# Deformable layer: the 7x7 offset convolution by even and odd columns with a shared sum

## The chip, the core and the metric

The kernel runs on one core of a Trainium2 chip. The metric is the device time of one execution in microseconds (us). A core has four computing engines with a queue each: TensorE (PE: matmuls, with weight loads shown apart as PEld), VectorE (DVE), ScalarE (ACT) and GpSimd (POOL); the transfers here are issued by SyncE (SP) and run on 16 DMA engines. The engines run in parallel and wait for each other by semaphores.

## The reference

A net of four layers on x of shape (8, 384, 32, 32), all float32: a Mamba layer, a deformable convolution layer, a second Mamba layer with an MLP, and a layer of shifts with a small depthwise convolution. Each adds its result to its input. The change is in the second, which (cut) computes:

```python
def deform_block(x, ow, ob, dw, pw, pb, K):           # x: 8 x 128 x 32 x 32
    offsets = conv2d(x, ow, ob, K // 2)               # K*K taps -> 2*K*K channels
    out = deform_depthwise(x, offsets, dw, K, K // 2) # sampled bilinearly at tap + offset
    return conv2d(out, pw, pb, 0)
c3, c5, c7 = split(group_norm(x), 3, axis=1)
out = concatenate([deform_block(c, ..., K) for c, K in ((c3, 3), (c5, 5), (c7, 7))], axis=1)
x = x + out * se_weight(out, fc1_w, fc2_w)
```

For K = 7 `conv2d` is a sum over 49 taps of a 128 x 98 weight matrix by the image moved by the tap, zero outside.

## The kernel before

The layers run one after the other. `deform_fast` (L918) does the deformable layer; a general version stands behind a branch on a flag (`far`) that says whether some offset was too large for the fast one.

For each of 8 samples it goes through three blocks, K = 3, 5, 7. A block has its taps in groups of four ("quads") and one single tap, each in two halves of the rows: 6, 14 and 26 units, 46 a sample. A unit samples by matmuls: ACT builds from the positions the bilinear weights ("hats": `fhx`, `fhy`, `unit_hats`), DVE multiplies them into `fsm` (L1387, a ring of five buffers) and weighs the transposed image into `fxk` (L1370, `unit_dve`), and PE adds 16 products (or 4) into `wacc`[...] (L1417, `unit_pe`).

The order of PE, DVE and ACT is written out by hand, in slots, one for each unit. In slot u there stand, in this order: the positions that SP loads for unit u+4 (if it is a first half); what `put` has filed under `act0`, `pe0`, `dve0`; `begin` at a block's first unit (zeroes `wacc`); PE's products of unit u interleaved with DVE's weighing and products of unit u+1; ACT's hats of unit u+2; and what is filed under `act1`, `dve1`, `pe1`. SP's and POOL's orders are left to a scheduler. Slots are numbered from 0 to 45 within a sample here: K = 3 is 0 to 5, K = 5 is 6 to 19, K = 7 is 20 to 45.

`block_steps` (L1033) files the rest of the work. What matters here:

- The offset convolution (`conv`, L1094) of K = 7 makes two halves of 16 rows x 32 columns, 49 taps each, seven taps a slot in slots 0 to 6 and 8 to 14, into `ps_off`, one bank. `offsets` (L1111), at slots 7 and 15, adds biases and grid on DVE, stores the positions to DRAM (`fposd`), and reduces maximum and minimum into `far`. For K = 3 and 5 the images lie in four and two strips of partitions, with one `offsets` each; the conv of the next sample's K = 3 is at slot 32 and of its K = 5 at slots 33 to 38.
- `load` (L1047) fetches the next sample's x into `fxn` (one buffer, all three groups) from slot 20, `stats`, `mean`, `dev`, `mean2`, `rstd` and `norm` normalize it in place in slots 22 to 31. `mean` (PE, L133) is under `pe0` of slot 25, the last of `stats` with the aggregate (L125) under `dve1` of slot 24.
- Before a block, `image` (ACT, L1147) copies its x into 4 x 8 cells (`fxc`); `cells` (DVE, L1152), four times, repeats them fourfold into `frep`; `cells_pe` (L1158) transposes them and `cells_act` (L1163) copies the result into `fxt`, a ring of six. `rows_pe` (L1133) transposes the plain rows.
- At a block's end `sums_act` (L1169 to L1172) closes `wacc` and copies two of its banks to `fdsb` on ACT, `sums` (L1177) adds the others on DVE, and only then may `begin` (L1298) zero `wacc` again. `pe0` stands between them.
- After a sample `residual` and `scale` load x into `fxr` (one buffer), add the scaled result and store it (L1227, L1231, L1232), in three parts.

Of the kernel before, what the change touches and what calls it, by code (L numbers as in the profile page):

```python
# [8 lines left out]
F32 = mybir.dt.float32  # L9
AF = mybir.ActivationFunctionType  # L10
ALU = mybir.AluOpType
AX = mybir.AxisListType
# [3 lines left out]
P = 128  # L16
C = 384
G = C // P
H = W = 32
L = H * W  # L20
HL = L // 2
# [18 lines left out]
NT = L // P  # L40
# [5 lines left out]
RAD = {3: 2, 5: 3, 7: 4}  # L46
CONV = {3: (4, 32, L // 4), 5: (2, 64, HL), 7: (1, P, L)}
NX = 4
NB = 5
HXN, HYN, SMN = 2080, 1792, 896  # L50


# [32 lines left out]
class Net:  # L85
# [832 lines left out]
    def deform_fast(self, src, dst):  # L918
        tc, nc, ins = self.tc, self.nc, self.ins
        with ExitStack() as ctx:  # L920
            wp = ctx.enter_context(tc.tile_pool(name="w1f", bufs=1))
# [5 lines left out]
            for g, K in enumerate(KS):  # L927
                K2, (n, st, cols) = K * K, CONV[K]
                rows = 2 * K2
                ow = wp.tile([P, K2, rows if n == 1 else st], F32, name=f"fow{K}")  # L930
                ob = wp.tile([P, 1], F32, name=f"fob{K}")
                obk = wp.tile([P, 1], F32, name=f"fobk{K}")
                grid = wp.tile([P, cols], F32, name=f"fgrid{K}")
                for t in (ob, obk, grid) + ((ow,) if n > 1 else ()):
                    nc.gpsimd.memset(t, 0.0)
                nc.sync.dma_start(out=ow[:, :, :rows], in_=ins[f"ow{K}"])
                for i in range(n):
                    r = slice(i * st, i * st + rows)
                    nc.sync.dma_start(out=ob[r], in_=ins[f"ob{K}"])
                    nc.sync.dma_start(out=obk[r], in_=ins["c_cols"][:rows, Q_K + g : Q_K + g + 1])  # L940
                    nc.sync.dma_start(out=grid[r], in_=ins["c_grid"][:rows, i * cols : (i + 1) * cols])
                nc.vector.tensor_tensor(obk, obk, ob, ALU.add)
                nq = K2 // 4
                wk = wp.tile([P, nq + 1, P], F32, name=f"fwk{K}")
                for t in range(4):
                    nc.sync.dma_start(
                        out=wk[H * t : H * (t + 1), :nq, :],
                        in_=ins[f"dw{K}"][t : 4 * nq : 4, :].partition_broadcast(H),
                    )
                nc.sync.dma_start(out=wk[:, nq, :], in_=ins[f"dw{K}"][4 * nq, :].partition_broadcast(P))  # L950
                self.f[K] = (ow, ob, obk, grid, wk)
# [23 lines left out]
            first = {}  # L975
# [18 lines left out]
            with tc.manual_schedule(engines=engines):  # L994
                for u in range(min(slots), max(slots) + 1):

                    def unit(i):
                        return units[i] if 0 <= i < len(units) else None

                    now, after, hats, grid = (unit(u + k) for k in (0, 1, 2, 4))  # L1000
# [21 lines left out]
            ps = self.psum("ps_bad", rows=1, n=1)  # L1022
# [7 lines left out]
        return bass.AP(tensor=ap.tensor, offset=ap.offset + off, ap=[list(ap.ap[0])] + [list(d) for d in dims])  # L1030


    def block_steps(self, b, g, first, put, weights, src, dst):  # L1033
        nc, K = self.nc, KS[g]
        K2, pad = K * K, K // 2
        n, st, cols = CONV[K]
        ow, ob, obk, grid, _ = self.f[K]
        pwt, pwb, f1, f2 = weights
        s = {}
        if g == 0:  # L1040
            s["sample"] = {}
        sample = s["sample"] = s["sample"] if g == 0 else self.state[b, 0]["sample"]
        s0 = first[b, g]
# [37 lines left out]
        def xg():  # L1081
            return sample["xn"][:, g, :]
# [2 lines left out]
        taps = [(0, 0)] + [  # L1085
            (y, x) for y in range(-pad, pad + 1) for x in range(-pad, pad + 1) if (y, x) != (0, 0)
        ]
        nh = 2 if n == 1 else 1
        m = HL if n == 1 else cols
        rows = m // W  # L1090
        width = 2 * K2 if n == 1 else st
        used = width * n

        def conv(h, t0, t1):  # L1094
            x3 = xg().rearrange("p (h w) -> p h w", w=W)
# [43 lines left out]
            for q in range(2):  # L1139
                nc.scalar.copy(xt[:, 4 * q : 4 * q + 4, :].rearrange("p t c -> p (t c)"), s["tr"][q])  # L1140

        def image():

            xc = s["xc"] = self.q1.tile([P, NT, NX, 4, 8], F32, name="fxc")
            x5 = xg().rearrange("p (by yl bx xl) -> p by yl bx xl", yl=4, bx=NX, xl=8)
            for yl in range(4):
                nc.scalar.copy(xc[:, :, :, yl, :], x5[:, :, yl, :, :])  # L1147

        def cells(q):
            rep = s["rep"] = self.q1.tile([P, 2 * NX, 4, 32], F32, name="frep")  # L1150
            xc = s["xc"].rearrange("p by bx yl xl -> p (by bx) (yl xl)")[:, 8 * q : 8 * q + 8, :]
            nc.vector.tensor_copy(rep, xc.unsqueeze(2).to_broadcast([P, 2 * NX, 4, 32]))  # L1152

        def cells_pe():
            s["tr"] = [self.psum("ps_t") for _ in range(2)]
            for i in range(2 * NX):
                a = s["rep"][:, i].rearrange("p t l -> p (t l)")
                nc.tensor.transpose(s["tr"][i // NX][:, i % NX * P : (i % NX + 1) * P], a, self.ident)  # L1158

        def cells_act(q):  # L1160
            xt = s[q] = self.q1.tile([P, 2 * NX, P], F32, name="fxt4", tag="fxt4", bufs=6)
            for by in range(2):
                nc.scalar.copy(xt[:, NX * by : NX * (by + 1), :].rearrange("p t c -> p (t c)"), s["tr"][by])  # L1163


        def sums_act():
            acc = s["acc"]
            for o in range(NB):
                nc.tensor.matmul(acc[:, o, :], self.zero[:, :P], self.zero, start=False, stop=True)  # L1169
            dsb = s["dsb"] = self.q1.tile([P, L], F32, name="fdsb")  # L1170
            nc.scalar.copy(dsb[:, :HL], acc[:, 0, :])
            nc.scalar.copy(dsb[:, HL:], acc[:, NB - 1, :])  # L1172

        def sums():
            for o in range(1, NB - 1):
                d = s["dsb"][:, 4 * o * W : 4 * o * W + HL]
                nc.vector.tensor_tensor(d, d, s["acc"][:, o, :], ALU.add)  # L1177
# [45 lines left out]
            nc.scalar.activation(sample["se"], sample["se"], AF.Sigmoid)  # L1223

        def residual(k):
            xr = sample["xr"] = self.q1.tile([P, L], F32, name="fxr")
            nc.sync.dma_start(out=xr, in_=src[:, k, :])  # L1227

        def scale(k):
# [3 lines left out]

        if g == 0:
            t = s0 - 2 * len(QUADS[KS[-1]])
            put(t, "act0", load)
            for i in range(G):
                put(t + 2 + i, "dve1", stats, i)
            put(t + 5, "pe0", mean)
            put(t + 5, "dve1", dev)  # L1240
            put(t + 6, "act1", square)
            put(t + 7, "pe0", mean2)
            put(t + 7, "dve1", var)
            put(t + 8, "act1", rstd)
            for i in range(G):
                put(t + 9 + i, "dve1", norm, i)
            put(t + 12, "pe1", conv, 0, 0, K2)
            put(t + 13, "dve0", offsets, 0)
        elif g == 1:
            t = first[b, 0] - 13  # L1250
            for i in range(6):
                put(t + i, "pe1", conv, 0, K2 * i // 6, K2 * (i + 1) // 6)
            put(t + 6, "dve0", offsets, 0)
        else:
            t = first[b, 0]
            for h in range(2):
                for i in range(7):
                    k = 8 * h + i
                    where = "pe0" if t + k in (first[b, 0], first[b, 1]) else "pe1"
                    put(t + k, where, conv, h, 7 * i, 7 * i + 7)  # L1260
                put(t + 8 * h + 7, "dve0", offsets, h)
        put(s0 - 4, "act0", image)
        put(s0 - 4, "pe1", rows_pe)
        put(s0 - 3, "act0", rows_act)
        put(s0 - 3, "dve0", cells, 0)
        put(s0 - 3, "pe1", cells_pe)
        put(s0 - 2, "act0", cells_act, 0)
        put(s0 - 2, "dve0", cells, 1)
        put(s0 - 2, "pe1", cells_pe)
        put(s0 - 1, "act0", cells_act, 1)  # L1270
        put(s0 - 1, "dve1", cells, 2)
        put(s0, "pe0", cells_pe)
        put(s0, "act1", cells_act, 2)
        put(s0, "dve1", cells, 3)
        put(s0 + 1, "pe0", cells_pe)
        put(s0 + 1, "act1", cells_act, 3)
        put(end, "act0", sums_act)
        put(end, "dve0", sums)
        put(end + 1, "pe1", point)
        put(end + 2, "act0", point_act)  # L1280
        put(end + 2, "dve1", squeeze)
        if g == G - 1:
            put(end + 3, "pe0", fc1)
            put(end + 3, "act1", relu)
            put(end + 4, "pe0", fc2)
            put(end + 4, "dve1", branches)
            put(end + 5, "act1", sigmoid)
            for k, t in enumerate((6, 9, 12)):
                put(end + t - 2, "act0", residual, k)
                put(end + t, "dve1", scale, k)  # L1290
        return s
# [112 lines left out]
    def unit_pe(self, b, g, j, half):  # L1404
# [344 lines left out]
```

## Time and profile before

Three runs took 9,599.3, 9,603.1 and 9,605.7 us. The profiled execution took 9,605.4 us; its trace spans 9,603.5.

| | us | what |
|---|---|---|
| median of 3 runs | 9,603.1 | |
| profiled execution / its span | 9,605.4 / 9,603.5 | mean TensorE clock 0.948 of full |
| deformable layer | about 3,058 to 5,970 | from the last store of the first layer's results |
| one sample in it | 355.3 | samples 1 to 6 lie between 355.1 and 356.7 |
| PE / DVE / ACT / POOL busy | 8,576 / 8,106 / 6,509 / 5,760 | over the span |

How to read it: the page has busy shares in 40 slices of 240 us, then groups of instructions by source line (busy us, mean ns of one, and the idle time before them with what ended it). A float32 matmul stands as two records, each with its own weight load. Matmuls overlap their neighbours, so their durations add up to more than the time they take; the time from one start to the next is what counts in a full queue. In the windows a row gives a stretch, its length, and the busy us and instructions of PE, PEld, DVE, ACT and POOL, then the granted clock, the DMA share and GB/s.

### The profile page before, as it was taken

How to read it: one execution, taken by the hardware profiler on the slowest of the kernel's cores; microseconds unless marked ns; L12 is line 12 of the kernel's file. 1: busy time of each engine (PE TensorE's matmuls, PEld its weight loads, DVE VectorE, ACT ScalarE, POOL GpSimd, SP SyncE). 2: the span in 40 equal slices, each digit the busy share in tenths (PEclk: the TensorE clock that was granted, in tenths of full speed). 3: DMA queues.
4: the chain of work that ended last, by engine and by line, in shares of the span. 5: the costliest groups of instructions: out<-in, count | busy, mean ns of one | idle time of the engine just before them, and what ended most of it. 6: DMA issues, size and time to landing. Idle time of an engine off the chain costs nothing. (4 is left out here: it accounts for less than half of the span.)

```text
span 9603.5 us, 87989 instructions
## 1 busy us (share of the span) xinstructions
PE 8576.2 (89%) x28252; PEld 4549.0 (47%) x28252; DVE 8106.0 (84%) x8807; ACT 6509.3 (68%) x10236; POOL 5760.4 (60%) x3788
## 2 busy tenths in 40 slices
PE   7898888888886899999999997699999999999987
PEld 2333333333332677677677676233433434433333
DVE  6999999999996678778778778699999999999983
ACT  5666666666663677777777777567777677777750
POOL 6888888888896000000000000699999999999974
PEclk8999999999998999999999999799999999999998
DMA  1211211121121233333333333233332243323336
GB/s 71 84 59 46 84 52 52 50 83 55 49 80 39 76 76 86 91 77 84 88 82 84 88 77 78 75 99 117 95 92 91 88 132 98 96 90 91 114 104 128
DMA packets 560754, 792.02 MB, mean 82 GB/s; under 512 B 238018, under 2 KB 391010, under 8 KB 536600
## 3 DMA queue, kind: packets, MB, share of 16 engines
q1 hardware_dynamic: 508056, 779.99, 27.7%
q10 hardware_dynamic: 52224, 6.30, 0.4%
q8 instruction: 225, 3.69, 0.2%
q14 instruction: 249, 2.04, 0.1%
HBM read 716.49 MB, written 69.66 MB: 82 GB/s over the span
## 5 line engine op out<-in xcount | busy, mean ns | idle before, releaser
L426 POOL TENSOR_TENSOR db<-du,bc 128x1024 f32<-128x1024 f32 x1536 | 3610.8, 2356 | 417.9 <-DVE hs L436 225.9
L436 DVE TENSOR_TENSOR_SCAN da<-da,db 128x1024 f32<-128x1024 f32 x1272 | 2912.3, 2290 | 200.3 <-ACT da L421 150.5
L467 PE MATMUL y<-hs,ident 128*128 128x512 f32 x5184 | 2613.1, 640 | 388.0 <-DVE hs L450 243.6
L421 ACT ACTIVATE da<-dt,na 128x512 f32<-128x512 f32 x3072 | 2119.9, 691 | 911.8 <-DVE hs L450 684.9
L394 POOL TENSOR_TENSOR dt<-dt,sp_e 128x512 f32<-128x512 f32 x192 | 244.1, 1271 | 3086.9 <-DVE sp_e L386 3086.9
L467 PEld LDWEIGHTS y<-hs,ident 128*128 128x128 f32 x5184 | 1019.6, 203 | 1879.1 <-issue 1142.7
L1417 PE MATMUL wacc<-fsm,fxk 128*128 128x221 f32 (+34 forms) x10624 | 1635.3, 312 | 73.3 <-DVE fsm L1387 71.5
L450 DVE TENSOR_TENSOR hs<-da,bc 128x1024 f32<-128x1024 f32 x1272 | 1557.9, 1225 | 118.5 <-PE y L467 14.1
L1417 PEld LDWEIGHTS wacc<-fsm,fxk 128*128 128x128 f32 x10624 | 1549.3, 193 | 209.2 <-DVE fsm L1387 132.5
L1387 DVE TENSOR_TENSOR fsm<-fhy,fhx 128x170 f32<-128x170 f32 (+42 forms) x3216 | 1173.2, 429 | 429.1 <-PE wacc L1417 413.7
L1347 ACT ACTIVATE fhy<-fpyx,cell 128x416 f32<-128x416 f32 (+9 forms) x1280 | 645.6, 576 | 397.7 <-DVE fsm L1387 397.7
L1105 PE MATMUL ps_off<-fxn,fow 128*32 128x248 f32 (+18 forms) x2944 | 831.8, 522 | 3.8 <-issue 2.0
L1370 DVE TENSOR_TENSOR fxk<-fxt,fwk 128x1024 f32<-128x1024 f32 (+1 forms) x688 | 786.6, 1180 | 6.4 <-ACT fxt L1163 6.4
L436 DVE TENSOR_TENSOR_SCAN hs<-da,db 128x1024 f32<-128x1024 f32 x264 | 602.4, 2282 | 69.0 <-POOL db L414 30.7
L447 POOL TENSOR_TENSOR hs<-hs,bc 128x1024 f32<-128x1024 f32 x264 | 622.1, 2357 | 36.6 <-ACT st L442 36.4
L454 POOL TENSOR_TENSOR hs<-hs 128x512 f32<-128x512 f32 x480 | 609.5, 1270 | 3.5 <-DVE hs L450 3.5
L550 PE MATMUL ps_m<-hid,wm 128*128 128x512 f32 x1152 | 536.7, 611 | 30.7 <-ACT hid L543 25.8
L528 PE MATMUL ps_h<-t,wm 128*128 128x512 f32 x1152 | 534.5, 601 | 17.0 <-DVE x L557 16.8
L1352 ACT ACTIVATE fhy<-fhy,cols 128x1344 f32<-128x1344 f32 (+10 forms) x368 | 530.7, 1442 | 12.0
L1105 PEld LDWEIGHTS ps_off<-fxn,fow 128*98 128x98 f32 (+2 forms) x2944 | 352.3, 147 | 381.6 <-issue 358.6
L442 ACT COPY st<-da 128x2 f32<-128x2 f32 x624 | 97.9, 157 | 506.3 <-DVE hs L450 504.8
L1334 ACT ACTIVATE fhx<-fpyx,cell 128x544 f32<-128x544 f32 (+8 forms) x640 | 380.1, 666 | 0.0
(192 smaller groups left out, 9453.3 us busy)
## 6 DMA issues: line engine op xcount, KB each, us to landing
bc<-bcd SPq DMA_DIRECT2D x256, 1024.0 KB
fpyx<-fposd SPq DMA_DIRECT2D x640, 256.0 KB
wm<-in_w SPq DMA_DIRECT2D x96, 768.0 KB
x<-x SPq DMA_DIRECT2D x71, 768.0 KB
winr<-in_win SPq DMA_DIRECT2D x192, 192.0 KB
x<-in_x SPq DMA_DIRECT2D x40, 768.0 KB
fpyx<-fposd SPq DMA_DIRECT2D x24, 1024.0 KB
wm<-in_wout SPq DMA_DIRECT2D x48, 384.0 KB
```

What stands on the lines that cost most here:

```text
L421: nc.scalar.activation(da[:, i, :], s["dt", j], AF.Exp, scale=na[:, j, n : n + 1])
L426: nc.gpsimd.tensor_tensor(db, du, s["bc"][m][:, 0], ALU.mult)
L436: nc.vector.tensor_tensor_scan(h1, da1, db1, 0.0, ALU.mult, ALU.add)
L447: nc.gpsimd.tensor_tensor(s["hs", m], s["hs", m], c, ALU.mult)
L450: nc.vector.tensor_tensor(hs, s["da", m], c, ALU.mult)
L454: nc.gpsimd.tensor_tensor(hs[:, 0, :], hs[:, 0, :], hs[:, 1, :], ALU.add)
L467: nc.tensor.matmul(s["y"], self.ident, s["hs", m][:, i, :], start=first and i == 0, stop=k == NU - 1 and i == n - 1,)
L1105: nc.tensor.matmul(o[:, ya - r0 : yb - r0, xa:xb], ow[:, (dy + pad) * K + dx + pad, :], x3[:, ya + dy : yb + dy, xa + dx : xb + dx], start ...
L1347: nc.scalar.activation(hy[:, at : at + (yb - ya) * W], pyx[:, 0, ya * W : yb * W], AF.Abs, bias=bias)
L1370: nc.vector.tensor_tensor(t[:, :n], x, wk[:, j : j + 1, :].to_broadcast([P, n, P]), ALU.mult)
L1387: nc.vector.tensor_tensor(self.sub(sm, at, [(r * w, n), (w, r), (1, w)]), self.sub(hy, hy_at[by] + xa, [(r * W, n), (W, r), (1, w)]), self ...
L1417: nc.tensor.matmul(a[:, ya - 4 * o : yb - 4 * o, xa:xb], k, self.sub(sm, sm_at[by], [(w, yb - ya), (1, w)]), start=False, stop=False,)
```

## The change

Write an image row as even columns e(i) = x(2i) and odd ones o(i) = x(2i+1), each 16 long. A row of seven weights on them gives two sums, for even and odd output columns, of seven half-row products each. They are rewritten with s(i) = e(i) + o(i): products of s with three weights serve both outputs, and four products with differences of weights complete the odd columns, four the even ones. Eleven products of 16 columns for each of seven tap rows, over all 32 rows at once, in three parts: 21 matmuls on the sum, 28 on odd columns, 28 on even columns of x, all into one bank in turn. After the first part ACT copies the sum with the bias to `ffs`; after each other part DVE adds it and writes every other column of `fpos`. `fir_end` reduces `far` from `fpos` (two reductions of 1,024), POOL adds the grid (with the tap added into it once at the start), and one store goes to DRAM. Six differences of weights are formed on POOL at the start (`fir_weights`), where seven DMAs fetch the weights in place of one.

Beside this: `image` is gone and `cells` reads `fxn` with two copies of half the size; `fxt` has four buffers; `fxr` shares `fdsb`'s buffer; the load, `mean` to `norm` and the convs of K = 3 and K = 5 stand a slot later, `stats` where it was; the three `scale` steps are at slots 5, 10, 13 in place of 6, 9, 12. In the order that the scheduler gives SP, the `fxn` load stood ahead of the positions of unit 22 and stands behind those of unit 24 now.

```diff
+NFIR = 11
+FIR = (
+    ((0, 1), (-1, 0), (1, 2)),
+    ((0, 6), (-2, 3), (-1, 7), (1, 9)),
+    ((0, 5), (-1, 10), (1, 8), (2, 4)),
+)
...
-                ow = wp.tile([P, K2, rows if n == 1 else st], F32, name=f"fow{K}")
+                ow = wp.tile([P, K * NFIR if n == 1 else K2, rows if n == 1 else st], F32, name=f"fow{K}")
...
-                nc.sync.dma_start(out=ow[:, :, :rows], in_=ins[f"ow{K}"])
+                if n == 1:
+                    self.fir_weights(ow, ins[f"ow{K}"])
+                else:
+                    nc.sync.dma_start(out=ow[:, :, :rows], in_=ins[f"ow{K}"])
...
+                if n == 1:
+                    nc.gpsimd.tensor_scalar(grid[:rows], grid[:rows], obk[:rows], None, ALU.add)
                 nc.vector.tensor_tensor(obk, obk, ob, ALU.add)
...
+    def fir_weights(self, ow, src):
+        nc = self.nc
+        w = ow.rearrange("p (y k) o -> p y k o", k=NFIR)
+        v = src.rearrange("p (y x) o -> p y x o", x=7)
+        for k, x in enumerate((1, 3, 5, 0, 6, 2, 4)):
+            nc.sync.dma_start(out=w[:, :, k, :], in_=v[:, :, x, :])
+        for d, i, j in ((7, 5, 0), (8, 6, 2), (9, 4, 2), (10, 3, 0), (5, 5, 1), (6, 6, 1)):
+            nc.gpsimd.tensor_tensor(w[:, :, d, :], w[:, :, i, :], w[:, :, j, :], ALU.subtract)
...
+        def fir_sum():
+            xs = s["xs"] = self.q1.tile([P, H, W // 2], F32, name="fxs")
+            x4 = xg().rearrange("p (h i e) -> p h i e", e=2, i=W // 2)
+            nc.vector.tensor_tensor(xs, x4[:, :, :, 0], x4[:, :, :, 1], ALU.add)
+
+        def fir(part, t0, t1):
+            if t0 == 0:
+                s["ps"] = self.mm.tile([P, HL], F32, name="ps_off", tag="conv", bufs=1)
+            x4 = xg().rearrange("p (h i e) -> p h i e", e=2, i=W // 2)
+            x3 = (s["xs"], x4[:, :, :, 1], x4[:, :, :, 0])[part]
+            o = s["ps"][:used].rearrange("p (h i) -> p h i", i=W // 2)
+            work = [(dy, d, k) for dy in (0, -3, -2, -1, 1, 2, 3) for d, k in FIR[part]]
+            for t in range(t0, t1):
+                dy, d, k = work[t]
+                ya, yb = max(0, -dy), min(H, H - dy)
+                xa, xb = max(0, -d), min(W // 2, W // 2 - d)
+                nc.tensor.matmul(
+                    o[:, ya:yb, xa:xb], ow[:, (dy + pad) * NFIR + k, :],
+                    x3[:, ya + dy : yb + dy, xa + d : xb + d], start=(t == 0), stop=(t == len(work) - 1),
+                )
+
+        def fir_take(part):
+            ps = s["ps"][:used]
+            if part == 0:
+                s["fs"] = self.q1.tile([P, HL], F32, name="ffs")
+                nc.scalar.activation(s["fs"][:used], ps, AF.Identity, bias=ob[:used])
+                return
+            if part == 1:
+                s["pos"] = self.q1.tile([P, cols], F32, name="fpos", tag="fpos")
+            pos = s["pos"][:used].rearrange("p (i e) -> p i e", e=2)[:, :, part - 1]
+            nc.vector.tensor_tensor(pos, ps, s["fs"][:used], ALU.add)
+
+        def fir_end():
+            pos = s["pos"][:used]
+            for e, (op, sign) in enumerate(((ALU.max, 1.0), (ALU.min, -1.0))):
+                k = 8 * b + 2 * g + e
+                fc = self.far[:used, k : k + 1]
+                nc.vector.tensor_reduce(fc, pos, AX.X, op)
+                nc.vector.tensor_scalar(fc, fc, sign / RAD[K], None, ALU.mult)
+            nc.gpsimd.tensor_tensor(pos, pos, grid[:used], ALU.add)
+            s["posd"] = self.dram.tile([2 * K2, L], F32, name="fposd", tag=f"posd{K}")
+            nc.sync.dma_start(out=s["posd"], in_=pos)
...
         def cells(q):
-            rep = s["rep"] = self.q1.tile([P, 2 * NX, 4, 32], F32, name="frep")
-            xc = s["xc"].rearrange("p by bx yl xl -> p (by bx) (yl xl)")[:, 8 * q : 8 * q + 8, :]
-            nc.vector.tensor_copy(rep, xc.unsqueeze(2).to_broadcast([P, 2 * NX, 4, 32]))
+            rep = s["rep"] = self.q1.tile([P, 2, NX, 4, 4, 8], F32, name="frep")
+            x5 = xg().rearrange("p (by yl bx xl) -> p by bx yl xl", yl=4, bx=NX, xl=8)
+            for by in range(2):
+                x = x5[:, 2 * q + by].unsqueeze(2).to_broadcast([P, NX, 4, 4, 8])
+                nc.vector.tensor_copy(rep[:, by], x)
...
-            xt = s[q] = self.q1.tile([P, 2 * NX, P], F32, name="fxt4", tag="fxt4", bufs=6)
+            xt = s[q] = self.q1.tile([P, 2 * NX, P], F32, name="fxt4", tag="fxt4", bufs=4)
...
-            xr = sample["xr"] = self.q1.tile([P, L], F32, name="fxr")
+            xr = sample["xr"] = self.q1.tile([P, L], F32, name="fxr", tag="fdsb")
...
-            put(t, "act0", load)
+            put(t + 1, "act0", load)
             for i in range(G):
                 put(t + 2 + i, "dve1", stats, i)
-            put(t + 5, "pe0", mean)
+            put(t + 6, "pe0", mean)
...
             t = first[b, 0]
-            for h in range(2):
-                for i in range(7):
-                    k = 8 * h + i
+            put(t - 1, "dve1", fir_sum)
+            k = 0
+            for part, pieces in enumerate((4, 5, 5)):
+                nw = K * len(FIR[part])
+                for i in range(pieces):
                     where = "pe0" if t + k in (first[b, 0], first[b, 1]) else "pe1"
-                    put(t + k, where, conv, h, 7 * i, 7 * i + 7)
-                put(t + 8 * h + 7, "dve0", offsets, h)
-        put(s0 - 4, "act0", image)
+                    put(t + k, where, fir, part, nw * i // pieces, nw * (i + 1) // pieces)
+                    k += 1
+                put(t + k, "dve0" if part else "act0", fir_take, part)
+            put(t + k, "dve0", fir_end)
...
-            for k, t in enumerate((6, 9, 12)):
+            for k, t in enumerate((5, 10, 13)):
```

More of the change, by code (lines that the diff above doesn't have):

```diff
@@ L1087, in block_steps @@
         ]
-        nh = 2 if n == 1 else 1
-        m = HL if n == 1 else cols
+        m = cols
         rows = m // W
@@ L1140, in rows_act @@
                 nc.scalar.copy(xt[:, 4 * q : 4 * q + 4, :].rearrange("p t c -> p (t c)"), s["tr"][q])
[L1142 to L1147, printed above, removed]
-        def cells(q):
-            rep = s["rep"] = self.q1.tile([P, 2 * NX, 4, 32], F32, name="frep")
-            xc = s["xc"].rearrange("p by bx yl xl -> p (by bx) (yl xl)")[:, 8 * q : 8 * q + 8, :]
-            nc.vector.tensor_copy(rep, xc.unsqueeze(2).to_broadcast([P, 2 * NX, 4, 32]))
+        def cells(q):
+            rep = s["rep"] = self.q1.tile([P, 2, NX, 4, 4, 8], F32, name="frep")
[3 more added lines that the diff above has]
+                nc.vector.tensor_copy(rep[:, by], x)
         def cells_pe():
@@ L1156, in cells_pe @@
             for i in range(2 * NX):
-                a = s["rep"][:, i].rearrange("p t l -> p (t l)")
+                a = s["rep"][:, i // NX, i % NX].rearrange("p t y x -> p (t y x)")
                 nc.tensor.transpose(s["tr"][i // NX][:, i % NX * P : (i % NX + 1) * P], a, self.ident)
         def cells_act(q):
-            xt = s[q] = self.q1.tile([P, 2 * NX, P], F32, name="fxt4", tag="fxt4", bufs=6)
+            xt = s[q] = self.q1.tile([P, 2 * NX, P], F32, name="fxt4", tag="fxt4", bufs=4)
             for by in range(2):
@@ L1169, in sums_act @@
                 nc.tensor.matmul(acc[:, o, :], self.zero[:, :P], self.zero, start=False, stop=True)
-            dsb = s["dsb"] = self.q1.tile([P, L], F32, name="fdsb")
+            dsb = s["dsb"] = self.q1.tile([P, L], F32, name="fdsb", tag="fdsb")
             nc.scalar.copy(dsb[:, :HL], acc[:, 0, :])
@@ L1235, in block_steps @@
             t = s0 - 2 * len(QUADS[KS[-1]])
-            put(t, "act0", load)
+            put(t + 1, "act0", load)
             for i in range(G):
                 put(t + 2 + i, "dve1", stats, i)
-            put(t + 5, "pe0", mean)
[L1240 to L1244, printed above, removed]
+            put(t + 6, "pe0", mean)
+            put(t + 6, "dve1", dev)
+            put(t + 7, "act1", square)
+            put(t + 8, "pe0", mean2)
+            put(t + 8, "dve1", var)
+            put(t + 9, "act1", rstd)
             for i in range(G):
-                put(t + 9 + i, "dve1", norm, i)
-            put(t + 12, "pe1", conv, 0, 0, K2)
-            put(t + 13, "dve0", offsets, 0)
+                put(t + 10 + i, "dve1", norm, i)
+            put(t + 13, "pe1", conv, 0, 0, K2)
+            put(t + 14, "dve0", offsets, 0)
         elif g == 1:
-            t = first[b, 0] - 13
+            t = first[b, 0] - 12
             for i in range(6):
```

## The prediction, made before the changed kernel ran

> **What bounds the kernel now.** I began with the page's busy shares by time slice. The deformable layer fills slices 14 to 25 (3,100 to 5,970 us); there the POOL row is 0 and the PE row almost always 9, with DVE at 7 or 8.
>
> ```profile
> PE   7898888888886899999999997699999999999987
> DVE  6999999999996678778778778699999999999983
> ACT  5666666666663677777777777567777677777750
> L1105 PE MATMUL ps_off<-fxn,fow 128*32 128x248 f32 (+18 forms) x2944 | 831.8, 522 | 3.8 <-issue 2.0
> ```
>
> An average of 9 can hide stages of different kinds. The layer repeats every 355.3 us, once a sample (first L1417 product of sample 2 at 3872.2, of sample 3 at 4227.5), in 46 slots of the hand-written order. So I cut one sample into five windows, along the slots: 0 to 14 (all 7x7 offset taps), 15 to 19, 20 to 31, 32 to 39 (offset convs of the next sample), 40 to 45. Columns: window, length, busy us of PE, PE loads, DVE, ACT, POOL.
>
> ```profile
> 3865.00:4005.30 140.30, 138.80 (x672) 89.44 (x671) 85.66 (x167) 94.37 (x150) 0.00 (x0) 1.00 0.32 84
> 4005.30:4040.00 34.70, 29.39 (x206) 25.81 (x205) 32.02 (x68) 29.10 (x43) 0.00 (x0) 0.96 0.48 143
> 4040.00:4117.30 77.30, 65.90 (x385) 61.06 (x383) 69.86 (x142) 67.60 (x95) 0.00 (x0) 0.93 0.29 69
> 4117.30:4184.20 66.90, 66.77 (x428) 51.97 (x429) 53.45 (x109) 53.53 (x70) 0.00 (x0) 1.00 0.34 83
> 4184.20:4220.30 36.10, 33.78 (x222) 32.11 (x222) 35.73 (x75) 30.01 (x47) 0.00 (x0) 1.00 0.23 61
> ```
>
> The reader is to see an alternation: PE is full in the first and fourth window with DVE at 61% and 80%, and DVE ends the second, third and fifth. The whole 7x7 offset conv stands in the first, where only PE counts.
>
> Next, what one tap costs. Durations (mean 522 ns) overlap, so I use start-to-start times of the weight loads in the timeline (first column the start): records of 464 columns follow each other after 0.39 us, of 512 after 0.43 us.
>
> ```profile
> 3955.13 0.16 PEld L1105 LDWEIGHTS ps_off<-fxn,fow 128*98 128x98 f32 x1 [0.23 <-issue]
> 3955.52 0.16 PEld L1105 LDWEIGHTS ps_off<-fxn,fow 128*98 128x98 f32 x1 [0.23 <-issue]
> 3957.97 0.17 PEld L1105 LDWEIGHTS ps_off<-fxn,fow 128*98 128x98 f32 x1 [0.26 <-issue]
> 3958.40 0.17 PEld L1105 LDWEIGHTS ps_off<-fxn,fow 128*98 128x98 f32 x1 [0.26 <-issue]
> ```
>
> That is 1.2 columns a nanosecond, and a matmul has two records (14 for 7 taps), so a tap costs 2 x columns / 1.2 ns; the load (0.17 us) hides under it.
>
> Last, the groups of instructions over 3,200 to 5,900 us and DVE's timeline in the third window.
>
> ```profile
> L133 PE MATMUL gn_ps<-gn_mv,gmat 128*128 128x2 f32 x126 | 27.8, 352 | 38.9 <-DVE gn_mv L125 38.9
> L1152 DVE COPY frep<-fxc 128x1024 f32<-128x1024 f32 x90 | 61.8, 686 | 7.8 <-PE ps_t L1158 7.8
> L1147 ACT COPY fxc<-fxn 128x256 f32<-128x256 f32 x88 | 28.8, 399 | 0.0
> ```
>
> ```profile
> 4072.59 0.34 DVE L125 BATCH_NORM_AGGREGATE gn_mv<-gn_st 128x2 f32<-128x12 f32 x3
> 4079.05 1.12 DVE L1387 TENSOR_TENSOR fsm<-fhy,fhx 128x171 f32<-128x171 f32 x2 [3.06 <-PE wacc L1417]
> 4081.56 1.12 DVE L1387 TENSOR_TENSOR fsm<-fhy,fhx 128x171 f32<-128x171 f32 x2 [1.39 <-PE wacc L1417]
> ```
>
> The first line is one hole a sample: PE sits 38.9 / 7 = 5.6 us before `mean`, which waits for the DVE aggregate of the slot before, although DVE is the late engine there. DVE then starves for 3.06 + 1.39 + 0.35 = 4.8 us behind PE.
>
> [...]No matmul of before reads its moving operand with a step[...]. [...]L1152 copies 1,024 elements in 686 ns, L1370 multiplies 1,024 in 1,218.
>
> **The change part by part.** Slots are those of one sample.
>
> *Taps.* Before, the columns of all 49 taps over both halves are (sum of 32-|dy|) x (sum of 32-|dx|) = 212 x 212 = 44,944 in 98 matmuls, 74.9 us at the rate above. After, each tap row has 11 products on 16 columns; the three shared have 16+15+15, the four each of odd and even 60, so 212 x 166 = 35,192 in 77 matmuls, 58.7 us. Saved: 16.3 us a sample. But the taps also spread otherwise: over slots 0 to 13 in place of 0 to 6 and 8 to 14. Slot 14 held seven taps (4.7 us), slot 7 none (now 4.6). So slots 0 to 13 win 16.3 - 4.7 = 11.6 us plus the roughly 0.3 us of PE idle at slot 7, say 11.9, all on the path (DVE and ACT have less to do in every one of them; I added them up).
>
> *Handing over.* Slot 14 is now PE's 3.9 us of products, against DVE's take (0.69, a 512-element tensor_tensor as L1177), two reduces of 1,024 (1.21 each, as L1196), two small ones (0.21), then weighing and products of the next unit, 5.1 us. All wait for the last tap, as `offsets(1)` did one slot later. So the DVE-bound stretch begins a slot earlier. Before: 8.6 us (slot 14 on PE) + 34.7 = 43.3. After: DVE's 32.0, less the old `offsets` (4006.16 to 4008.52, 2.4), plus 3.3, plus 5.1, plus 0.3 for cells, plus the same 2.7 idle = 41.0. Gain 2.3. Slots 0 to 19 together: 14.2 us for each of 8 samples = 113.6.
>
> *Other waits.* The take of the shared sum waits on ACT at slot 4, with hats two units ahead queued behind; of the odd columns on DVE at slot 9, with 2.8 us of weighing and first product behind it against some 5 us of products that PE still has. Hidden. The sum of even and odd (0.69 us, slot 45) lies before a PE stretch; hidden. POOL's add (2.36 us by L426, whose neighbour on DVE, L450, takes 1,225 ns beside it against 1,218 for L1370 with POOL idle, so no contention) and one store come 10 us after slot 13, well before slot 18 needs the positions. On SP, the store and the loads of `fxr`, now in the buffer of `fdsb`, move by a slot; the first store must land before `sums_act` of slot 6, whose DVE work ended 3.1 us ahead of PE's taps (4.0 us now instead of 5.9, so 1.2 left). Hidden, narrowly.
>
> *Cells.* Four copies of 1,024 a block become eight of 512, directly from `fxn`: about 0.42 us each by the rate of L1152, 0.08 of it overlapping, so +0.1 us a cell, twelve a sample, eight of them in DVE windows: under 1 us. L1147 (1.3 us of ACT a block) goes; ACT ends no window, so nothing. Unknown: whether the 8-element runs keep the double rate. Between +0.1 and +0.6 us a cell; I take +0.1[...]. The `fxt` ring of four in place of six: each buffer's last weighing is a slot or more ahead of its refill; nothing.
>
> *Statistics a slot later.* `mean` goes to slot 26, after PE's products of slot 25; its 4 us then fall in time that PE waits for DVE anyway. Bounds: 0 to 5.6 us; I take 4.5, the DVE starvation less a cell. The 3x3 conv shifts from slot 32 to 33 and the 5x5 by one: slot 32 becomes DVE-bound (6.9 us against PE's 5.3), about -1.5 by slot 40, and -0.3 for cells at the end. Net +2.7 for 7 samples = 19. The `fxn` load now waits for the last cell copy (about 4040.6) and follows one more set of positions on SP, where it was issued at 4016.3. At startup it landed 6.8 us after issue; statistics begin at 4057.5. No stall, some 7 us to spare.
>
> *Start, once.* Seven weight DMAs of 392-byte runs for one: 3,200 packets of 200 bytes took 3.8 us here, the old weights 9 us; so 6,272 packets take 8 to 11. Six POOL subtractions of 686 (about 1.6 us each between L394's 1.27 for 512 and L426's 2.36 for 1,024) and the grid add follow, and DVE's bias add, in front of the statistics, waits for them: ready near 3,101 to 3,106 against 3101.0. Cost -1 to 12 us; I take 3.
>
> Sum: 113.6 + 19 - 3 = 130 us from the profiled execution's 9,605 us (span 9,603.5, 2 us around it; the median of the runs is 9,603.1, practically the same). Forecast 9,474.
>
> **Rivals.**
> *Strided reads at half speed (slower).* If the matrix engine takes the step-2 operands at half rate, 2 x 60/166 of the 58.7 us doubles: +42.4 us a sample, 339 in all: 9,813. For it: no such read stands in the trace. Against: [...]fp32 records already take only 1.2 columns a nanosecond. It decides from a slowdown of 38% of those records (16.2 / 42.4). Chance 0.09.
> *Cells at single rate.* +0.5 us x 8 cells x 8 samples = 33: 9,507. For it: the four-level source. Chance 0.10.
> *A new wait takes part of it back.* A late `fxn`, the `fdsb` buffer, or `mean` merely moving its wait: 5 to 8 us a sample, 40 to 65 in all: 9,515 to 9,540. For it: three margins of a few us. Chance 0.17.
> *All idle closes.* Taps entirely won (16.3 x 8) plus 5.6 x 7: 170, so 9,435. Chance 0.05, as DVE would have to be faster than its sum.
>
> **How the numbers follow.** Forecast 0.58, rivals 0.09, 0.10, 0.17, 0.05, and 0.01 for no visible change. The range, 9,432 to 9,540, takes in all but the strided rival and tails. A measurement tells changes over 0.2% (19 us). Faster 0.89, same 0.02, slower 0.09.
>
> **What would show it.** The 7x7 records should follow each other after columns / 1.2 ns also for the two strided parts (0.43 us at 512); 0.6 or more would be the slow rival. The first window should shrink from 140 to about 120 us (to the end of slot 13), DVE should be full right after; `gn_ps<-gn_mv` should have no idle before it; the copies to `frep` should take near 0.42 us; sample time about 338 us. A sample time above 345, or `gn_st` waiting for the `fxn` load, would make the prediction wrong.

## The result, and the profile after

The changed kernel takes 9,658.8 us (median of 4 runs, 9,656.2 to 9,661.8) against 9,603.6 for the kernel before on the same chip (4 runs): 1.0058 times the time, 95% interval 1.0041 to 1.0076. It is slower by 55 us, where 9,474 was forecast. The profiled execution spans 9,656.4 us.

The page of the changed kernel shows a suspect, in a row that had no counterpart before. First the busy tenths of PE and POOL in 40 slices, then one group of instructions:

```profile
PE   7898888888886898898898898589999999999987
...
POOL 6888888888895101101101101599999999999974
...
L1158 POOL TENSOR_TENSOR fpos<-fpos,fgrid 98x1024 f32<-98x1024 f32 x8 | 244.1, 30508 | 2504.8 <-DVE far L1156 2504.8
```

The unbroken run of nines that PE had in the deformable layer is now a beat of 8, 9, 8, and POOL, which was at 0 there, shows a 1 in two slices of three. The only work POOL has there is its new add of the grid, and each of the eight adds lasts 30.5 us. The forecast had 2.36.

Cut along the same slots as before (sample 2; slots 0 to 13, 14 to 19, 20 to 31, 32 to 39, 40 to 45), first the kernel before, then the changed one. Columns: window, length, busy us of PE, PE loads, DVE, ACT, POOL, granted clock, DMA share, GB/s.

```profile
3872.21:3997.40 125.19, 123.69 (x599) 79.65 (x598) 77.75 (x153) 83.85 (x130) 0.00 (x0) 1.00 0.33 86
3997.40:4039.95 42.55, 37.24 (x250) 31.66 (x249) 34.44 (x74) 32.91 (x50) 0.00 (x0) 0.97 0.39 117
...
sum 355.30, PE 334.63 PEld 260.40 DVE 276.70 ACT 274.60 POOL 0.00; mean PE 66.93 PEld 52.08 DVE 55.34 ACT 54.92 POOL 0.00
```

```profile
3884.89:4005.42 120.53, 117.18 (x575) 75.61 (x574) 74.94 (x150) 84.27 (x129) 0.00 (x0) 1.00 0.32 88
4005.42:4062.99 57.57, 34.75 (x234) 31.59 (x234) 38.31 (x81) 31.45 (x46) 30.51 (x1) 0.80 0.23 62
4062.99:4136.07 73.08, 65.17 (x386) 59.51 (x384) 69.25 (x143) 67.60 (x95) 0.00 (x0) 0.95 0.38 94
4136.07:4204.22 68.15, 66.98 (x429) 52.03 (x429) 54.64 (x114) 56.85 (x75) 0.00 (x0) 1.00 0.34 79
4204.22:4246.47 42.25, 40.17 (x244) 35.42 (x245) 40.57 (x84) 31.21 (x48) 0.00 (x0) 1.00 0.31 80
sum 361.58, PE 324.25 PEld 254.16 DVE 277.71 ACT 271.38 POOL 30.51; mean PE 64.85 PEld 50.83 DVE 55.54 ACT 54.27 POOL 6.10
```

PE's work did shrink, by 10.4 us a sample. But the second stage grew from 42.6 to 57.6 us while PE, DVE and ACT are each busy in it for under 39. The timeline of the changed kernel, all engines, at the end of that stage (start, duration, engine, line; in brackets the idle time before and what ended it):

```profile
4009.01 30.51 POOL L1158 TENSOR_TENSOR fpos<-fpos,fgrid 98x1024 f32<-98x1024 f32 x1 [331.47 <-DVE far L1156]
...
4036.62 0.69 DVE L1436 TENSOR_TENSOR fxk<-fxt,fwk 128x512 f32<-128x512 f32 x1
...
4039.55 0.31 SPq L1160 DMA_DIRECT2D fposd<-fpos  x1
...
4042.55 15.31 SPq L1384 DMA_DIRECT2D fpyx<-fposd  x9
...
4047.52 1.15 ACT L1400 ACTIVATE fhx<-fpyx,cols 128x1024 f32<-128x1024 f32 x1 [17.10 <-DMA fpyx<-fposd]
...
4053.30 1.76 DVE L1453 TENSOR_TENSOR fsm<-fhy,fhx 128x256 f32<-128x256 f32 x3 [15.99 <-ACT fhy L1418]
...
4055.54 1.94 PE L1221 MATMUL ps_t<-ident,frep 128*128 128x128 f32 x8 [16.15 <-DVE frep L1215]
```

Read it from the bottom. PE waits 16 us for DVE, DVE 16 us for ACT's hats, ACT 17 us for the positions, these for the store, and the store for POOL's add. And the add ends 2.21 us after DVE's last instruction before its pause (4037.31 to 4039.52). That distance is the same in all eight samples, and 2.2 us is about what such an add takes by itself. So POOL seems to have worked only once DVE had stopped, and DVE stopped only when it had nothing left but work that needed the add. That is a reading of one trace; the experiments test it.

Two smaller things. The stage of the taps, slots 0 to 13, won 4.7 us. Slot 0's taps run ahead of the first product, where the stage is cut here; they won another 0.9 us (4.85 us before, from 3866.28 to 3871.13; 3.98 now, from 3879.84 to 3883.82), which lie in the last row of these tables. The forecast for all taps was 11.9 us. Here are its matmuls in the changed kernel by form, on strided columns (`fxn`) and on the contiguous sum (`fxs`); durations overlap, so their differences count:

```profile
L1135 PE MATMUL ps_off<-fxn,fow 128*98 128x435 f32 x116 | 52.2, 571 | 0.0
...
L1135 PE MATMUL ps_off<-fxs,fow 128*98 128x435 f32 x56 | 23.9, 528 | 0.0
...
L1135 PE MATMUL ps_off<-fxn,fow 128*98 128x512 f32 x28 | 15.1, 620 | 0.0
...
L1135 PE MATMUL ps_off<-fxs,fow 128*98 128x512 f32 x14 | 7.2, 592 | 0.0
```

Start to start it is 451 ns against 429 for 512 columns and 409 against 366 for 29 rows of 15. And two steps went as forecast: no idle time stands before `mean` any more (38.9 us before), and the small copies to `frep` take 419 ns.

```profile
L1215 DVE COPY frep<-fxn 128x512 f32<-128x512 f32 x176 | 66.4, 419 | 7.8 <-PE ps_t L1221 7.8
...
L140 PE MATMUL gn_ps<-gn_mv,gmat 128*128 128x2 f32 x126 | 14.8, 249 | 0.0
```

### The profile page after: what moved, and what is told of

It is laid out like the page before. It is cut to its first block, busy times and chain, and to the rows that moved or that the text cites. A ratio compares the mean times of both kernels' runs of the same rounds, so it can differ in the third digit from the quotient of the medians.

```text
span 9656.4 us, 87414 instructions
## 1 busy us (share of the span) xinstructions
PE 8491.1 (88%) x27891; PEld 4504.2 (47%) x27916; DVE 8114.4 (84%) x8879; ACT 6482.8 (67%) x10148; POOL 6012.0 (62%) x3803
## 5 line engine op out<-in xcount | busy, mean ns | idle before, releaser
L1158 POOL TENSOR_TENSOR fpos<-fpos,fgrid 98x1024 f32<-98x1024 f32 x8 | 244.1, 30508 | 2504.8 <-DVE far L1156 2504.8
L457 DVE TENSOR_TENSOR hs<-da,bc 128x1024 f32<-128x1024 f32 x1272 | 1557.9, 1225 | 117.2 <-PE y L474 12.8
L1135 PE MATMUL ps_off<-fxn,fow 128*98 128x465 f32 (+10 forms) x896 | 386.6, 579 | 0.0
```

The source lines that it names most:

```text
L457: nc.vector.tensor_tensor(hs, s["da", m], c, ALU.mult)
```

## The experiments

In the texts of the first runs, A puts the length of the add on its own shape, B puts the loss elsewhere, and C puts it on what runs beside the add. All times are medians; the kernel before took 9,605.2 (12 runs), 9,607.6 and 9,605.4 us (7 runs each) beside the three groups of runs.

**The add on DVE.** One word of the changed kernel:

```diff
-            nc.gpsimd.tensor_tensor(pos, pos, grid[:used], ALU.add)
+            nc.vector.tensor_tensor(pos, pos, grid[:used], ALU.add)
```

> The grid add of K = 7 moves from POOL to DVE (one 98 x 1024 tensor_tensor, some 1.2 us in slot 14). Theory A, the loss is POOL's add, which took 30.5 us in place of the 2.4 forecast and holds the positions of slot 20 back: PE's hole at slot 19 falls from 19.9 us to about 3, the sample from 361.8 to about 346 us, the whole to about 9,530. Rival B, the loss is the single late store and SP's new order (store, positions, fxn behind each other): the add is only part of it and the whole stays above 9,620. Rival C, something in POOL's surroundings[...]: like A here.

Measured: 9,530.2 us, 0.9920 of before (0.9903 to 0.9936). The sample falls from 361.6 to 345.9 us, slots 14 to 19 from 57.6 to 40.5. So that one instruction, on an engine with nothing else to do, cost 129 us and the whole sign of the change. B, which had the whole above 9,620 us, falls. The run leaves open why the add is slow on POOL.

**All 128 partitions.** The add over the whole tile, rows 96 to 127 filled before (`fpos` and the grid have 128):

```diff
+                nc.gpsimd.memset(s["pos"][96:], 0.0)
...
-            nc.gpsimd.tensor_tensor(pos, pos, grid[:used], ALU.add)
+            nc.gpsimd.tensor_tensor(s["pos"], s["pos"], grid, ALU.add)
```

> POOL still adds the grid, but over all 128 partitions of the tile in place of 98 (the rest set to zero by POOL before). Theory A, the number of partitions makes it slow: the add takes about 2.4 us as every 128 x 1024 add of the layers around does, sample about 345 us, whole about 9,522. Rival C, the surroundings ([...]the operands) make it slow: still about 30 us, whole about 9,655. Rival B: add fast, whole above 9,620.

Measured: 9,656.8 us, 1.0053 (1.0036 to 1.0070). The group of instructions in this kernel:

```profile
L1159 POOL TENSOR_TENSOR fpos<-fpos,fgrid 128x1024 f32<-128x1024 f32 x8 | 244.0, 30497 | 1267.2 <-DVE far L1157 1267.2
```

30.5 us again: the odd number of 98 partitions has nothing to do with it.

**The add in three pieces.**

```diff
-            nc.gpsimd.tensor_tensor(pos, pos, grid[:used], ALU.add)
+            for r in (slice(0, 64), slice(64, 96), slice(96, used)):
+                nc.gpsimd.tensor_tensor(pos[r], pos[r], grid[r], ALU.add)
```

> POOL's add over 98 partitions in three pieces: 64, 32 and 2 partitions. Theory A in its first form (a partial group of 32 is slow): the first two take 2.4 us each, the piece of 2 some 30 us, whole about 9,690. Theory A in its second form (only a count that is not a multiple of 16 or 32 beyond the first group): all three near 2.4 us, 7 us together, whole about 9,555. Rival C: all three near 30 us, 90 together, whole far above 10,000.

Measured: 9,694.5 us (one run). POOL's groups by form in this kernel:

```profile
L1159 POOL TENSOR_TENSOR fpos<-fpos,fgrid 64x1024 f32<-64x1024 f32 x8 | 244.0, 30502 | 2506.7 <-DVE far L1156 2506.7
L1159 POOL TENSOR_TENSOR fpos<-fpos,fgrid 2x1024 f32<-2x1024 f32 x8 | 18.7, 2336 | 0.5
L1159 POOL TENSOR_TENSOR fpos<-fpos,fgrid 32x1024 f32<-32x1024 f32 x8 | 18.6, 2331 | 0.5
```

None of the expectations had this: the time is near the 9,690 of A's first form, but by luck, as another piece is the slow one. The first piece takes all of the 30.5 us, the two others 2.3 each, for 32 and for 2 partitions alike. The shape can't explain that; an order in time can: the first piece waits for DVE's pause, and the others run inside it. That turns theory C into a sharper one, D: while DVE issues instructions back to back, POOL's add doesn't start at all.

**DVE stands still for the add.** The direct test of D. The add stays on POOL, and DVE gets an instruction behind it that needs its result:

```diff
             nc.gpsimd.tensor_tensor(pos, pos, grid[:used], ALU.add)
+            nc.vector.tensor_copy(s["fs"][:used, :1], pos[:, :1])
```

> The changed kernel with its add of the grid left on POOL, and behind it one more instruction on DVE that copies a single column of the sum (98x1, into a buffer that is dead by then), so that DVE has to stand still until POOL's add has ended. Theory D (POOL's add is kept off as long as DVE issues its products and copies one behind the other, and needs only some 2.3 us once DVE stands still): although a wait is added to DVE's queue, the add falls from 30.5 us to between 2.2 and 2.6, the idle time of PE in slot 19 goes, and the whole falls to about 9,540: the 9,530 of the add on DVE, and some 1.2 us more a sample because DVE waits 2.4 us where it would work 1.2. Rival E (the add is slow on POOL by itself, or because of PE, ACT or the DMAs): the add stays near 30 us, DVE stands still for all of it, and the whole is 9,700 or more.

Measured: 9,537.3 us, 0.9929 (0.9912 to 0.9945). The timeline of this kernel, first POOL, then DVE:

```profile
3969.18 2.34 POOL L1158 TENSOR_TENSOR fpos<-fpos,fgrid 98x1024 f32<-98x1024 f32 x1 [344.29 <-DVE far L1156]
...
3969.08 0.15 DVE L1157 TENSOR_SCALAR far<-far 98x1 f32<-98x1 f32 x1
3971.55 0.15 DVE L1159 COPY ffs<-fpos 98x1 f32<-98x1 f32 x1 [2.32 <-POOL fpos L1158]
3971.62 2.35 DVE L1437 TENSOR_TENSOR fxk<-fxt,fwk 128x1024 f32<-128x1024 f32 x2
```

The same add on the same data takes 2.34 us. The other engines do not explain the difference. Here are the 2.34 us of this add, and then the first 2.34 us of the add in the changed kernel (columns as in the windows above):

```profile
3969.18:3971.52 2.34, 0.49 (x5) 0.29 (x3) 0.05 (x1) 0.00 (x0) 2.34 (x1) 1.00 0.00 0
```

```profile
4009.01:4011.35 2.34, 0.50 (x5) 0.30 (x3) 2.34 (x4) 0.00 (x0) 2.34 (x1) 1.00 0.00 0
```

PE does as much in both, ACT and the transfers do nothing; only DVE differs. In the first stretch the add is done, in the second 28 us of it are still to come. A wait of 2.3 us a sample, added on the busiest engine of this stage, makes the kernel 121 us faster. E falls, D stands.

**Small adds on POOL.** From the kernel with the add on DVE, with thirteen adds of 98 x 64 a sample, whose result nobody reads:

```diff
+        def probe():
+            nc.gpsimd.tensor_tensor(s["fs"][:used, :64], grid[:used, :64], grid[:used, :64], ALU.add)
...
+            for i in range(16, 42, 2):
+                put(t + i, "dve0", probe)
```

> The kernel with the grid's add on DVE, and thirteen adds of 98x64 on POOL a sample, in slots 16, 18 to 40, of the grid's first 64 columns into a buffer that is dead by then; nothing waits for them. Theory D: those that fall among unbroken work of DVE last several us, up to the next gap of DVE, although they have only a sixteenth of the columns (some 0.2 us of work); those in a gap last well under 1 us; the sums of DVE's own instructions don't grow, and the whole stays at 9,530 within 10. Rival F (the two share the memory in turns, instruction by instruction): each lasts no more than one DVE instruction, about 1.2 us, and DVE's products grow somewhere. Rival G (only large adds suffer, by bytes): all last 0.2 to 0.6 us.

Measured: 9,530.7 us (0.9919, 0.9902 to 0.9936), as without them. They did not spread over the slots: nothing held POOL back, and it began all thirteen right behind the last take of slot 14. This makes the test stricter, as the small adds now follow each other without a break. POOL's timeline in this kernel in two windows (the second shows the eighth add alone), and DVE's over the same stretch:

```profile
3971.55 2.53 POOL L1152 TENSOR_TENSOR ffs<-fgrid 98x64 f32<-98x64 f32 x7 [311.13 <-DVE fpos L1149]
...
3974.15 31.88 POOL L1152 TENSOR_TENSOR ffs<-fgrid 98x64 f32<-98x64 f32 x1
```

```profile
3971.44 1.22 DVE L1159 TENSOR_REDUCE far<-fpos 98x1 f32<-98x1024 f32 x1
3972.69 0.15 DVE L1160 TENSOR_SCALAR far<-far 98x1 f32<-98x1 f32 x1
3972.76 1.21 DVE L1159 TENSOR_REDUCE far<-fpos 98x1 f32<-98x1024 f32 x1
3974.01 0.15 DVE L1160 TENSOR_SCALAR far<-far 98x1 f32<-98x1 f32 x1
3974.08 1.22 DVE L1161 TENSOR_TENSOR fpos<-fpos,fgrid 98x1024 f32<-98x1024 f32 x1
...
4005.14 0.74 DVE L1218 COPY frep<-fxn 128x512 f32<-128x512 f32 x2
4007.67 2.13 DVE L1243 TENSOR_TENSOR fdsb<-fdsb,wacc 128x512 f32<-128x512 f32 x3 [1.79 <-ACT fdsb L1238]
```

While DVE reduces, which is one input from SBUF, POOL does seven adds in 2.53 us, 0.29 each. DVE's add at 3974.08 is its first instruction with two inputs in SBUF; the eighth of POOL's adds begins 0.07 us later and ends at 4006.03, 0.15 us after DVE's last copy (4005.88). So 0.29 us of work took 31.9, G falls, and so does F: not one of DVE's instructions between them let POOL in, and DVE lost nothing (its first eight products into `fsm` after that take 2.89 us together, and also 2.89 in the kernel where DVE stands still, with POOL idle beside them). Up to 3990.70 every one of these instructions has two inputs in SBUF. Later ones are also copies to `frep`; the last two of them, alone, kept POOL off for another 0.7 us.

**Contiguous columns.** For the missing part of the tap stage. From the kernel with the add on DVE; ACT copies the odd, then the even columns into `fxs`, and all three parts read that:

```diff
+        def fir_copy(part):
+            xs = s["xs"] = self.q1.tile([P, H, W // 2], F32, name="fxs")
+            x4 = xg().rearrange("p (h i e) -> p h i e", e=2, i=W // 2)
+            nc.scalar.copy(xs, x4[:, :, :, 2 - part])
...
-            x3 = (s["xs"], x4[:, :, :, 1], x4[:, :, :, 0])[part]
+            x3 = s["xs"]
...
+                if part < 2:
+                    put(t + k, "act0", fir_copy, part + 1)
```

> The grid's add on DVE as in the run before, and the 7x7 convolution's second and third parts read a contiguous copy of the odd and of the even columns, which ACT makes in slots 4 and 9 into the buffer of the shared sum (two copies of 128x512 more a sample). Theory S (PE's 5 to 12% longer matmuls in these parts come from reading every second column): 512 columns fall from 451 to 429 ns, 15 rows of 29 from 409 to about 366, some 4.2 us a sample, and the whole goes from 9,530 to about 9,497. Rival (they come from the short rows of 13 to 15 columns or from what else is on the memory in these slots): the durations stay, and the whole is 9,530 to 9,540.

Measured: 9,505.8 us, 0.9895 (0.9879 to 0.9912), 24 us less than with strided reads, where 33 were expected. The 435-column form in this kernel, all of it from `fxs`:

```profile
L1139 PE MATMUL ps_off<-fxs,fow 128*98 128x435 f32 x172 | 70.9, 528 | 0.0
```

528 ns, where the strided ones took 571: the stride was the cause. Slots 0 to 13 win 3.5 us of the 4.2 expected, and ACT pays 1.3 us a sample for its copies (660 ns each).

**The end by halves.** From the last kernel; each take is followed by its own two reductions and its own add of half the grid:

```diff
             nc.vector.tensor_tensor(pos, ps, s["fs"][:used], ALU.add)
+            for e, (op, sign) in enumerate(((ALU.max, 1.0), (ALU.min, -1.0))):
+                k = 8 * b + 2 * (g + part - 1) + e
...
+            gr = grid[:used].rearrange("p (i e) -> p i e", e=2)[:, :, part - 1]
+            nc.vector.tensor_tensor(pos, pos, gr, ALU.add)
```

> The kernel with contiguous columns, and the end of the convolution taken by halves: the extreme values and the grid's add of the odd output columns at slot 9, behind their sum, and only those of the even columns at slot 14, all on DVE. Slot 14 then has some 1.8 us less on the path from the last matmul to the positions (half of two reductions of about 1.2 us and of an add of 1.2), and slot 9 that much more, beside products of PE. If slot 14's chain still sets the start of the windows: about 9,497 - 8 x 1.8 = 9,483. If it doesn't, or slot 9 now stalls PE: 9,495 to 9,505.

Measured: 9,486.2 us, 0.9872 (0.9855 to 0.9888), 20 us less, where 14 were expected. The chain of slot 14 does set the start of the windows.

**Products at the block boundaries.** From the last kernel:

```diff
-                    where = "pe0" if t + k in (first[b, 0], first[b, 1]) else "pe1"
+                    where = "pe0" if t + k - first[b, 0] in (0, 1, 6, 7) else "pe1"
```

> The kernel with contiguous columns and halves, and the convolution's products of slots 1 and 7 go to PE ahead of the slot's window products and of the pointwise matmuls, as those of slots 0 and 6 do already. Theory H (what is still missing of the forecast lies at the block boundaries, where PE now waits for ACT to empty ps_t: 0.97 us before the pointwise matmuls in slot 1 and 0.81 in slot 7, with fewer products ahead of them than before): both waits go, 1.8 us a sample, and the whole falls from 9,486 to about 9,472. Rival (ACT is the bound of these slots, so the wait only moves to the products that follow): 9,483 to 9,488.

Measured: 9,469.5 us (9,467.3 to 9,473.1), 0.9862 of before (0.9846 to 0.9879), 17 us less than without this edit. PE's waits over slots 0 to 7 of sample 2 (who waits, for whom, us in total, times, longest), in the kernel before, then without the edit and with it:

```profile
PE ps_pw L1183 <- ACT fxt L1163: 1.5, 2, 1.0
```

```profile
PE ps_t L1226 <- ACT fxt L1231: 1.9, 2, 1.3
PE ps_pw L1251 <- ACT fxt L1231: 1.8, 2, 1.0
```

```profile
PE ps_t L1226 <- ACT fxt L1231: 1.9, 2, 1.3
```

The wait before the pointwise matmuls is gone. But 1.5 of its 1.8 us stood in the kernel before too, so most of this is a new gain, and not time that the change had lost. What the change did add is the wait for `ps_t`, and it stays. This version beats both kernels: 136 us under before, 189 under the change as it was.

**The statistics a slot later, alone.** The kernel before with `mean` to `norm` and the convs of K = 3 and K = 5 a slot later, and nothing else:

```diff
-            put(t + 5, "pe0", mean)
+            put(t + 6, "pe0", mean)
...
-            t = first[b, 0] - 13
+            t = first[b, 0] - 12
```

> The kernel before, with only the mean, the normalization and the 3x3 and 5x5 offset convs one slot later (stats and load stay). If this part works as forecast, the 5.6 us hole of PE before the mean goes and about 3 us a sample are won for 7 samples: 9,580 (9,565 to 9,595). Rival: the time comes back in the later slots and nothing is won, 9,603.

Measured: 9,582.1 us (9 runs), 0.9977 (0.9967 to 0.9987), 23 us less.

## Why the prediction was wrong

The sample in us by stages, as forecast by the prediction's steps and as measured (sample 2):

| slots | before | forecast | changed | add on DVE | all edits |
|---|---|---|---|---|---|
| 0 to 13 | 125.2 | 114.2 | 120.5 | 120.5 | 114.6 |
| 14 to 19 | 42.6 | 40.2 | 57.6 | 40.5 | 39.1 |
| 20 to 45 | 187.6 | 184.0 | 183.5 | 184.9 | 186.0 |
| sum | 355.3 | 338.4 | 361.6 | 345.9 | 339.7 |

Of the 11.9 us forecast for the taps, 0.9 stands in the third row here, for slot 0. Samples 1 to 6 of one kernel differ by up to 2.4 us (with all edits they take 338.0 to 340.0). Forecast and outcome are 23.2 us a sample apart, 185 in all.

- **The step that failed** is the sentence on POOL: "POOL's add (2.36 us by L426, whose neighbour on DVE, L450, takes 1,225 ns beside it against 1,218 for L1370 with POOL idle, so no contention) ... come 10 us after slot 13". The duration was right for an add that is let in (2.34 us when DVE stood still). The inference was wrong, twice. L450 multiplies `da`, which stands in PSUM, by an operand in SBUF: one input from SBUF. Beside it POOL's add took 2.36 us; that is no evidence for the deformable layer, whose products and weighings take both inputs from SBUF. And the test looked at the wrong victim: DVE's 1,225 against 1,218 says that DVE isn't slowed; POOL is the one that loses. The add lasted as long as DVE's stream (30.5 us in place of 2.34): DVE's instructions overlap by some 0.08 us in the trace, and POOL got no turn between them for 28 us. Why it got none, no run shows. The prediction asked whether the two slow each other by a share; the question was who waits, and for how long.
- **It closed a loop.** An engine kept off for 30 us costs nothing if nobody needs it (with the small adds, one of which lasted 31.9 us a sample, the kernel took 9,530.7 us, without them 9,530.2). Here DVE would have stopped of itself at slot 18 or 19, for positions that needed the add, and only this stop let the add in. Behind it came all of the latency, store, load and hats: 16 us of idle DVE a sample. Slots 14 to 19 are 17.4 us over the forecast, and with the add on DVE 0.3.
- **The taps were mis-sized:** 11.9 us forecast, 5.5 measured (4.7, and 0.9 for slot 0). 3.5 of the missing 6.4 are the strided reads (contiguous columns). The other 2.9 were not tried one by one. With contiguous columns, PE's waits for ACT over slots 0 to 7 are 2.2 us longer than before: 1.9 for `ps_t`, which the kernel before doesn't have, and 0.3 before the pointwise matmuls. They are the likely part; some 0.7 us stay open. The prediction saw that the taps thin out per slot, but counted only PE's sum and not what they had covered at the boundaries, where PE waits for ACT.
- **Full speed for the strided reads** was the author's assumption, which no trace of before showed, and it didn't hold: start to start the reads at a step of two took 5% (451 ns against 429, 512 columns) to 12% (409 against 366, 29 rows of 15) longer. The rival of half speed, the one case that ended slower, had the cause of this right and its size wrong: 24 us, not 339. It was not the cause of the sign.
- **Handing over** was right as soon as the add was off POOL: 40.5 against 40.2, though DVE then spends 1.2 us on the add.
- **The statistics** were right in kind and near in size: slots 20 to 45 fall by 2.7 us with the add on DVE, of which 0.9 is slot 0's taps, so 1.8 where 2.7 were forecast; alone in the kernel before the move was worth 23 us, where the sum had 19 with the cells in it. The `fxn` load made nobody wait.
- **The start** cost 1.1 us of the 3 forecast: from the last store of the first layer's results to the first statistics it is 43.2 us before and 44.3 in the changed kernel.
- **Cells** went as forecast: 419 ns for 512 elements against 0.42 us, by the rate of before (686 ns for 1,024).
- **The new-wait rival** listed three margins (`fxn`, `fdsb`, `mean`) and passed over the fourth new dependence on the path, an engine that had been idle. None of its cases reached above the time before.

With the add on DVE and contiguous columns the kernel takes 9,505.8 us, 32 above the forecast. The version with all edits ends at 9,469.5 us and so reaches the forecast's sum, but by gains that the forecast did not count: the halves (20 us) and the products at the boundaries (17 us, most of it from a wait that the kernel before has too).

## What to carry to other kernels

Before work goes to an idle POOL, list what DVE runs at that time by the number of its inputs in SBUF, and its copies too: here products of two SBUF inputs, with copies to `frep` (419 ns for 512 elements) among them, made 30.5 us of an add of 2.34. A neighbour that reads PSUM proves nothing (beside L450 the add took 2.36 us). Look at both engines' durations, and ask whether DVE will itself come to wait for POOL's result: if so, the pause comes at the end of DVE's queue, with the whole latency behind it (here 16 us of idle DVE a sample). Work on a busy engine also covers that engine's waits for others: when it shrinks, look at each wait that it stood beside (here 1.5 us of new waits for `ps_t` a sample in the changed kernel).

## What the runs showed of the hardware that was not expected

- An add of 98 x 64 on POOL, 0.29 us in a gap of DVE, lasted 31.9 us beside back-to-back DVE instructions with two SBUF inputs and copies to `frep` (two in 0.74 us), and ended 0.15 us after the last of them. Beside one-input reductions on DVE seven such adds took 0.29 us each.
- In a trace this looks like a long POOL instruction, not like a wait: it starts at once, its duration holds the delay (30.5 us against 2.34).
- A wait of 2.3 us a sample put on DVE made the kernel 121 us faster.
- fp32 matmuls whose moving operand has a step of two take 451 ns from start to start against 429 (512 columns) and 409 against 366 (29 rows of 15).
- POOL's add of 1,024 columns takes 2.34, 2.33 and 2.34 us on 2, 32 and 98 partitions.
